# What runs in front of the first attention: masks before statistics, sums and differences on VectorE, the second half's sums within the loops, and another memory layout

## The chip, the cores and the metric

The kernel runs on one core of a Trainium2 chip. Its time is the device time in microseconds (us) of one execution. Three runs of the kernel before gave a median of 3515.47 us (3515.45 to 3517.23). Views of one profiled execution are quoted besides; the engines are PE (TensorE's matmuls; PEld its weight loads), DVE (VectorE), ACT (ScalarE), POOL (GpSimd) and SP (SyncE, which only issues DMAs here).

## The reference, cut to what matters

The whole program is a stack of layers on an image of 256 channels and 64 x 64 pixels: a group norm with a windowed linear attention (the part this document is about), a deformable convolution, two attentions and two mixtures of experts. The first attention computes, for 8 heads of 32 channels:

```
q = sigmoid(Wq x);  k = sigmoid(Wk x);  v = Wv x, each pixel's head vector divided by its length
Ik = integral image of k;  Ikv = integral image of k (outer product) v
for ws in 64, 32, 16:                # window of ws x ws pixels around each pixel, cut at the edge
    wk  = box(Ik, ws);  wkv = box(Ikv, ws)
    attn = q . wkv                   # 32 values per head and pixel
    norm = q . wk                    # one value per head and pixel
    outs.append(attn / (norm + 1e-6))
out = Wout concat(outs) + bout
```

x is the group-normalised image here.

## The kernel before, in words

Everything is done in two halves of 128 channels (4 heads), hf = 0 and 1. The image is cut into 8 blocks of 8 pixel rows (NBLK), 512 pixels each (NB).

*Masks* (`masks0`, line 248 on). Window membership is a product of a row vector and a column vector per mask. DVE computes the small vectors (`inside`, lines 282 and 283: two instructions per row or column of a mask), POOL multiplies them out to bf16 masks (lines 297, 301, 312, 327). `group_norm` (line 157 on) has DVE compute statistics of the image (16 `bn_stats`, line 166), a short chain of tiny operations over all engines gives mean and scale, and then DVE normalises the first 128 channels (line 172) and ACT the second (line 173) into y. Neither is in a hand-written order: a scheduler decides how the two mix on DVE.

*Preparation* (`prep0`, line 401 on), once per half, in an order written by hand for PE, DVE, ACT and POOL (`manual_schedule`):
- k of all 8 blocks: PE multiplies (line 146, a helper that all matmuls of this stage share), ACT applies the sigmoid twice, into the integral image T and into k (lines 413, 414), DVE scans along rows (line 422) and adds rows and blocks (line 418).
- a loop over the blocks nb. `ahead` takes T's row differences (line 478), window 16 on DVE and windows 64 and 32 on POOL. PE makes q of the next block and k and v of this one, pixels on partitions (kv); `keys` and `values` give v's length by ACT and DVE (lines 440 to 454). `weighed` takes column differences on DVE and multiplies by q (lines 496 to 501); `norms` sums them on PE into nrm (line 509). `tiles` multiplies k by v per tile of 8 x 8 pixels on PE, and ACT copies it to S (line 467). `sums` adds S over columns and rows on POOL, per block, with single 32- to 256-element additions (line 520), 10 to 16 per block.
- at the end, DVE takes the reciprocal of nrm (lines 566, 567); the sums go to DRAM (fard, neard; lines 548, 549), and the reciprocals too (recd, line 568).

POOL's sums of one half run until after its last block; DVE's reciprocal also.

*Attention* (`half0`, line 570 on), once per half, only PE's order written by hand. A first loop over u (8 columns of tiles, window 64) and a second over I (8 blocks). Per u it needs the state b from fard (block-diagonal tile bd, line 579, which must be zeroed once, line 383), the keys kt (kc, line 600), and v by columns (vt, line 377, 16 loads per half, from vd in DRAM). `region0` works through jobs, four for each u: PE multiplies scores (l_s, line 706) into six PSUM banks; of the four head products of a job DVE masks two straight from PSUM (line 718), ACT copies two (line 713) and POOL masks them with one multiplication (line 723); two jobs later PE multiplies them by vt (line 752), added to what the state gives (line 739).

Memory: the mask vectors' pool is freed before y's is made; y, the weights w_qk and w_kv, T and the constants share an area with what attention needs, so the weights are loaded, T's edges cleared and bd, vt loaded when the earlier users are through. SP and ACT issue the DMAs, each in its own order.

Of the kernel before, what the change touches and what calls it, by code (L numbers as in the profile page):

```python
# [88 lines left out]
class Net:  # L89
# [158 lines left out]
    def masks0(self, pool, tmp):  # L248
# [30 lines left out]
        def inside(out, d, at, ws):  # L279

            lo, hi = float(-(ws // 2) - at), float(ws // 2 - 1 - at)
            nc.vector.tensor_single_scalar(out, d, lo, ALU.is_ge)
            nc.vector.scalar_tensor_tensor(out, d, hi, out, ALU.is_le, ALU.mult)

        M = {}
        for ws, nr, n in ((32, 2, 10), (16, 1, 14)):
            rows = tmp.tile([P, 3, TR], F32, tag="rows", name="m_rows")
            cols = tmp.tile([P, 5, TCOL], F32, tag="cols", name="m_cols")
            for i, di in enumerate((-nr, 0, nr)):
                inside(rows[:, i], d_row, TR * di, ws)  # L290
            for j in range(5):
                inside(cols[:, j], d_col, TCOL * (1 - j % 3), ws)
            halves = cols.rearrange("p j (h c) -> p (j h) c", c=HC)
# [8 lines left out]


        rows = tmp.tile([P, 10, TR], F32, tag="rows10", name="m_rows")
        for i in range(10):
            inside(rows[:, i], d_tall, -TR * (i - 4), 64)
        cols = tmp.tile([P, 2, HC], F32, tag="cols2", name="m_cols")
        for s, du in enumerate((-4, 4)):
            inside(cols[:, s], d_half, HC * du, 64)
        full = pool.tile([P, 2, 10, TR, HC], BF16, tag="mask_c", name="mask_c")  # L310
        for s in range(2):
            nc.gpsimd.tensor_tensor(full[:, s], bc(rows, 3, HC), bc(bc(cols[:, s], 1, TR), 1, 10), ALU.mult)
        M["c"] = full.rearrange("p s i r c -> p s i (r c)")


        rows = tmp.tile([P, 2, TR], F32, tag="rows2", name="m_rows")
        for s, di in enumerate((-4, 4)):
            inside(rows[:, s], d_row, TR * di, 64)
        hf = tmp.tile([P, 1], F32, tag="hf", name="m_h")
        nc.vector.tensor_copy(hf, h_i)  # L320
        near = tmp.tile([P, 10], F32, tag="near", name="m_near")
        nc.vector.memset(near, 1.0)
        nc.vector.tensor_scalar(near[:, 0:2], hf.to_broadcast([P, 2]), 0.0, None, ALU.is_equal)
        nc.vector.tensor_scalar(near[:, 8:10], hf.to_broadcast([P, 2]), 0.0, None, ALU.is_gt)
        full = pool.tile([P, 2, 10, TR, HC], BF16, tag="mask_r", name="mask_r")
        for s in range(2):
            nc.gpsimd.tensor_tensor(full[:, s], bc(bc(rows[:, s], 1, 10), 3, HC), bc(bc(near, 2, TR), 3, HC), ALU.mult)
        M["r"] = full.rearrange("p s i r c -> p s i (r c)")
        return M

    def layer0(self, xc, x, xd, done):
# [4 lines left out]
        with tc.tile_pool(name="l0", bufs=1) as pool, tc.tile_pool(name="l0d", bufs=1, space=DRAM) as dpool:  # L336
# [7 lines left out]
            with tc.tile_pool(name="l0m", bufs=1) as tmp:  # L344
                M = self.masks0(pool, tmp)
            with tc.tile_pool(name="l0y", bufs=1) as ypool:
                y = ypool.tile([P, 2, N], F32, tag="y", name="l0_y")
                tiled = lambda a: a.rearrange("p (i u r c) -> p i r u c", i=NBLK, u=NU, r=TR)
                raster = lambda a: a.rearrange("p (i r u c) -> p i r u c", i=NBLK, r=TR, u=NU)
                self.group_norm(xc, lambda m: [(tiled(y[:, m])[:, i], raster(xc[:, m])[:, i]) for i in range(NBLK)])  # L350
                done()
                with (
                    tc.tile_pool(name="l0a", bufs=2) as wp,
                    tc.tile_pool(name="l0g", bufs=1) as gpool,
                    tc.tile_pool(name="l0a_ps", bufs=2, space=PSUM) as ps,
                ):
                    self.weights(ypool, ["w_qk0", "w_kv0"])
                    self.consts0(ypool)
                    T = gpool.tile([P, HW + 1, HW + 1], F32, tag="T", name="l0_T")
                    nc.gpsimd.memset(T[:, 0, :], 0.0)  # L360
                    nc.gpsimd.memset(T[:, 1:, 0:1], 0.0)
                    ET = mybir.EngineType
                    with tc.manual_schedule(engines={ET.PE, ET.DVE, ET.Activation, ET.Pool}):
                        for hf in range(2):
                            self.prep0(hf, y, q[hf], k[hf], None if hf else v, vd[hf], fard[hf], neard[hf], recd[hf], T, gpool, wp, ps)
            with (
                tc.tile_pool(name="l0o", bufs=1) as wop,
# [3 lines left out]
                vt = wop.tile([P, 4, NU, P], F32, tag="vt", name="l0_vt")  # L371

                def tall(hf):
                    by_rows = vd[hf].rearrange("(i b j) (h n) c -> b n i j h c", b=2, j=4, h=2)
                    for u in (4, 5, 6, 7, 0, 1, 2, 3):
# [3 lines left out]
                tall(0)  # L379
                self.weights(wop, ["w_out0"])  # L380
                bd = [[wp.tile([P, (NU, 4)[wi], P], F32, tag=f"bd{wi}{i}", name=f"l0_bd{wi}", bufs=1) for i in range(2)] for wi in range(2)]
                for b in bd[0] + bd[1]:
# [2397 lines left out]
```

## Time and profile before

| what | us |
|---|---|
| median of three runs | 3515.47 |
| the profiled execution | 3449.32 |
| its span, first to last instruction | 3447.3 |
| PE busy in the span | 3096.6 (90%) |
| DVE, POOL, ACT busy | 2302.0, 1566.5, 1319.1 |
| last statistic aggregated | 28.4 |
| first matmul of k | 35.2 |
| first S product of half 0, last one | 69.1, 130.9 |
| first S product of half 1, last one | 166.1, 227.2 |
| first score matmul of attention | 252.35 |

A line in order of time gives the start, the duration (of a run of equal instructions: from the first's start to the last's end), the engine, the line of the kernel, the operation, output <- inputs, the shapes and the count; in brackets stands how long the engine was idle just before, and what ended that. A line of windows gives, for a stretch, its length, each engine's busy time with its count of instructions, TensorE's granted clock (1.00 is full), the DMA engines' mean busy share and GB/s.

### The profile page before, as it was taken

To read this page: it belongs to the slowest core of one execution; us is meant where nothing else is said; L and a number is where in the kernel's file an instruction comes from. 1 tells how busy PE (TensorE), PEld (TensorE's weight loads), DVE (VectorE), ACT (ScalarE), POOL (GpSimd) and SP (SyncE) were. 2 spreads that over 40 slices of the span, in tenths; PEclk is the share of its full clock that TensorE was granted. 3 is DMA by queue.
4 is the path that set the end of the run, shared out by engine and by line. 5 is a ranking of instruction groups with operands and counts; after the bars stand their busy time and mean duration, and the time that the engine had idled before them with its cause. 6 is when DMAs were issued, how large, how long until landed. Compare 5 with 4: busy or idle time off the path is not lost.

```text
span 3447.3 us, 65631 instructions
## 1 busy us (share of the span) xinstructions
PE 3096.6 (90%) x25404; PEld 2321.3 (67%) x25404; DVE 2302.0 (67%) x5325; ACT 1319.1 (38%) x2537; POOL 1566.5 (45%) x1523
## 2 busy tenths in 40 slices
PE   5759999999977899797969789999999996999997
PEld 3433444344435888665857567888888885889996
DVE  7865776577764677797755576777777775555552
ACT  3435443443325666342533352222222222333331
POOL 3679887788752555443444352000000003555552
PEclk9879999999989999998979899999999997999998
DMA  1136655611134222200148653323333224555554
GB/s 68 43 90 143 173 151 154 156 52 52 52 110 123 61 74 74 57 1 1 56 166 264 214 192 123 103 87 96 101 99 98 90 64 158 195 193 203 206 203 174
DMA packets 241687, 406.97 MB, mean 118 GB/s; under 512 B 78353, under 2 KB 152850, under 8 KB 231890
## 3 DMA queue, kind: packets, MB, share of 16 engines
q1 hardware_dynamic: 212786, 345.19, 32.2%
q0 software_dynamic: 13056, 35.93, 2.7%
q10 hardware_dynamic: 15520, 21.52, 1.8%
q8 instruction: 204, 3.34, 0.4%
q14 instruction: 121, 0.99, 0.1%
HBM read 287.07 MB, written 111.30 MB: 116 GB/s over the span
## 4 chain that ended last, share of the span: by engine, by line
PE 40%; DVE 9%; DMA 5%; issue 5%; ACT 3%; POOL 3%; SPq 0%; DVEq 0%; POOLq 0%; ACTq 0%
PE a_sa_ps L2403 6%; PE f_h_ps L146 5%; DMA ys<-f_y,f_at 3%; PE a_oa_ps L2442 3%; PE a_ob_ps L2442 3%; PE a_oc_ps L2442 3%; PE a_sb_ps L2403 3%; PE f_ya_ps L146 2%; PE l_acc_ps L1097 2%; PE f_yb_ps L146 2%; PE a_od_ps L2442 1%; POOL ys L2158 1%; PE a_sc_ps L2403 1%; PE a_q_ps L146 1%; DVE l_pr L1093 1%
## 5 line engine op out<-in xcount | busy, mean ns | idle before, releaser
L713 ACT COPY l_sc<-l_s 128x384 f32<-128x384 f32 (+1 forms) x632 | 303.9, 532 | 459.9 <-PE l_s L706 434.2
L1971 POOL DMA_INDIRECT xs<-f_room,f_to x64 | 64.7, 1011 | 696.8 <-issue 582.2
L718 DVE TENSOR_TENSOR l_sm<-l_s,mask 128x256 f32<-128x256 f32 (+2 forms) x628 | 308.1, 552 | 91.2 <-PE l_s L706 90.3
L146 PE MATMUL f_h_ps<-f_xT,f_w 128*128 128x256 f32 x1440 | 339.8, 387 | 19.5 <-DVE f_xT L2078 9.6
L146 PEld LDWEIGHTS f_h_ps<-f_xT,f_w 128*128 128x128 f32 x1440 | 261.3, 191 | 83.1 <-ACT f_h L2088 31.8
L706 PE MATMUL l_s<-l_q,l_k 32*128 32x256 f32 (+3 forms) x2944 | 270.9, 453 | 0.0
L2422 ACT ACTIVATE a_e<-a_e 128x512 f32<-128x512 f32 x256 | 156.0, 629 | 243.2 <-DVE a_e L2392 237.9
L723 POOL TENSOR_TENSOR l_sm<-l_sc,mask 128x768 f32<-128x768 f32 (+1 forms) x116 | 202.8, 1755 | 87.7 <-ACT l_sc L713 87.5
L2088 ACT ACTIVATE f_h<-f_h_ps,f_w 128x256 f32<-128x256 f32 x360 | 166.3, 470 | 186.4 <-PE f_h_ps L146 177.1
L1093 DVE TENSOR_TENSOR l_pr<-l_vk,l_w_ps 128x1280 f32<-128x1280 f32 x128 | 186.6, 1482 | 54.1 <-PE l_acc_ps L1097 34.9
L706 PEld LDWEIGHTS l_s<-l_q,l_k 32*128 32x128 f32 x2944 | 132.7, 183 | 115.3 <-issue 68.3
L2158 POOL DMA_INDIRECT ys<-f_y,f_at x144 | 145.5, 1010 | 138.9 <-ACT f_y L2157 108.7
L1097 PE MATMUL l_acc_ps<-ident,l_pr 128*128 128x128 f32 x1600 | 198.1, 278 | 6.3 <-POOL l_pr L1088 6.2
L1097 PEld LDWEIGHTS l_acc_ps<-ident,l_pr 128*128 128x128 f32 x1600 | 184.7, 144 | 13.0 <-POOL l_pr L1088 7.8
L727 POOL TENSOR_TENSOR l_sm<-l_sc,mask 128x256 f32<-128x256 f32 (+1 forms) x220 | 184.8, 868 | 13.9 <-ACT l_sc L713 12.9
L2115 POOL TENSOR_TENSOR f_wt<-f_w 128x512 f32<-128x512 f32 x72 | 89.9, 1269 | 217.7 <-PE f_ya_ps L146 206.3
L2403 PE MATMUL a_sa_ps<-a_q,a_kt 128*128 128x256 f32 x512 | 155.8, 386 | 11.1 <-DVE a_u L2408 10.1
L2407 ACT COPY a_u<-a_sa_ps 128x256 f32<-128x256 f32 x128 | 47.6, 372 | 292.5 <-PE a_sa_ps L2403 292.5
L752 PE MATMUL l_b_ps<-l_sm,l_v 128*32 128x256 f32 (+2 forms) x2176 | 153.2, 372 | 0.0
L2403 PE MATMUL a_sa_ps<-a_qt,a_kt 128*128 128x256 f32 x512 | 152.7, 380 | 0.0
L723 POOL TENSOR_TENSOR l_sm<-l_sc,mask_c 128x768 f32<-128x768 f32 (+1 forms) x64 | 120.0, 1892 | 36.8 <-ACT l_sc L713 36.3
L2403 PE MATMUL a_sb_ps<-a_qt,a_kt 128*128 128x256 f32 x512 | 132.1, 381 | 0.0
(555 smaller groups left out, 7388.0 us busy)
## 6 DMA issues: line engine op xcount, KB each, us to landing
a_kt<-a_kd SPq DMA_DIRECT2D x128, 512.0 KB
f_w<-in_f_w SPq DMA_DIRECT2D x36, 1152.0 KB
f_w<-in_f_w SPq DMA_DIRECT2D x36, 1028.0 KB
xs<-zero SPq DMA_DIRECT2D x8, 4160.0 KB
l_vk<-vt SPq DMA_DIRECT2D x180, 128.0 KB
f_x<-xs SPq DMA_DIRECT2D x72, 260.0 KB
f_w<-in_f_w SPq DMA_DIRECT2D x36, 384.0 KB
l_rcp<-l_recd SPq DMA_DIRECT2D x48, 256.0 KB
```

The lines of the kernel that those rows point to most:

```text
L146: self.nc.tensor.matmul(out, lhsT, rhs, start=(i == 0), stop=(i == len(pairs) - 1))
L706: nc.tensor.matmul(s[pair, j][:, at : at + m, :], key(hp), qs[hp], start=(z == 0), stop=(z == len(pieces) - 1))
L713: nc.scalar.copy(sc[:, j], s[1, j])
L718: nc.vector.tensor_tensor(to(pair, j, kind, at), pick(s[pair, j], kind, which), mask, ALU.mult)
L723: nc.gpsimd.tensor_tensor(out[:, :, at, :], of[:, :, which, :], bc(mask, 1, 2), ALU.mult)
L727: nc.gpsimd.tensor_tensor(to(1, j, kind, at), pick(sc[:, j], kind, which), mask, ALU.mult)
L1093: nc.vector.tensor_tensor(pr, vk, bc(held["w"][:, j, dy], 3, D), ALU.mult)
L1097: nc.tensor.matmul(acc[:, m, j, :], pf[:, dx, m * P : (m + 1) * P], self.ident, is_transpose=True, start=(j == 0 and dy == 0 and dx == 0 a ...
L2088: nc.scalar.activation(h[:, m, :], q, AF.Gelu, bias=w1[:, 2 * hidden + m : 2 * hidden + m + 1])
L2158: nc.gpsimd.indirect_dma_start(out=self.ys_parts[(i % 4) * NI + k], in_=y[:, k, :], in_offset=None, out_offset=bass.IndirectOffsetOnAxis(a ...
L2403: mm = lambda out, i, right: nc.tensor.matmul(out, A[i], right, start=True, stop=True)
L2442: nc.tensor.matmul(out, vs[:, j, i, :], right, start=(j == 0 and side != 1), stop=(j == NPAIR - 1 and side != 0))
```

## The change

- The mask vectors are computed for several rows or columns at once (an index tile `x_i`, one `inside` with an outer sum), 48 DVE instructions in all, in a hand-written order in front of the statistics. POOL multiplies masks in another order (mask_c, mask_r, then 32 and 16). A dummy square root on ACT precedes everything.
- The weights have a pool of their own and are loaded at the start; T and the constants also have their own pools.
- In `prep0` all row differences are on DVE (before: two of three on POOL).
- `sums` becomes `sums0`: the same additions on DVE, for four blocks at a time: `columns(0)`, `columns(1)`, `rows`, `nears`. For half 0, `columns(0)` runs at block 5; the reciprocal and the other three run at the start of half 1's preparation. For half 1 all of them are handed on to attention (`more`), where the scheduler may place them: in the compiled order `columns(0)` stands within blocks 4 to 6 of the loop, and the rest on DVE before and between the masks of u = 0.
- k of half 1: the first four blocks are multiplied before the last S product of half 0 (`lead`), each gets one sigmoid, and ACT copies k into T.
- vt, bd and kc have a pool in y's old place; tiles of attention's second loop (rcp, o, xs) have one that is made when the sums' memory is free. One vt pair is loaded first, the rest and w_out in attention's first job. The sums' tiles stand at the other end of memory.

```diff
         for ws, nr, n in ((32, 2, 10), (16, 1, 14)):
...
-            for i, di in enumerate((-nr, 0, nr)):
-                inside(rows[:, i], d_row, TR * di, ws)
-            for j in range(5):
-                inside(cols[:, j], d_col, TCOL * (1 - j % 3), ws)
+            inside(rows, d_row, -TR * nr, TR * nr, ws)
+            inside(cols[:, :3], d_col, TCOL, -TCOL, ws)
...
-            with tc.tile_pool(name="l0m", bufs=1) as tmp:
-                M = self.masks0(pool, tmp)
...
+                self.weights(kpool, ["w_qk0", "w_kv0"])
...
-                self.group_norm(xc, lambda m: [(tiled(y[:, m])[:, i], raster(xc[:, m])[:, i]) for i in range(NBLK)])
+                with tc.tile_pool(name="l0m", bufs=1) as tmp, tc.manual_schedule(engines={ET.DVE, ET.Pool, ET.Activation}):
+                    root = tmp.tile([P, 1], F32, tag="root", name="m_root")
+                    nc.scalar.activation(root, self.one, AF.Sqrt)
+                    M = self.masks0(pool, tmp)
+                    self.consts0(kpool)
+                    T = tpool.tile([P, HW + 1, HW + 1], F32, tag="T", name="l0_T")
+                    nc.gpsimd.memset(T[:, 0, :], 0.0)
+                    nc.gpsimd.memset(T[:, 1:, 0:1], 0.0)
+                    self.group_norm(xc, lambda m: [(tiled(y[:, m])[:, i], raster(xc[:, m])[:, i]) for i in range(NBLK)])
                 done()
...
+                gpool = side.enter_context(tc.tile_pool(name="l0g", bufs=1, side="right"))
+                sums = self.sums0(gpool, fard, neard)
...
-                        for hf in range(2):
-                            self.prep0(hf, y, q[hf], k[hf], None if hf else v, vd[hf], fard[hf], neard[hf], recd[hf], T, gpool, wp, ps)
+                        lead = lambda: [self.channels0(1, y, k[1], i, C, ps) for i in range(4)]
+                        rest = self.prep0(0, y, q[0], k[0], v, vd[0], recd[0], T, sums, gpool, wp, ps, [], lead)
+                        rest = self.prep0(1, y, q[1], k[1], None, vd[1], recd[1], T, sums, gpool, wp, ps, rest, lambda: None)
...
+                        more = rest + [late] if hf == 0 else []
...
+        if hf == 1:
+            for i in range(4, NBLK):
+                channels(k, i, C)
+        for go in rest:
+            go()
         for i in range(NBLK):
-            channels(k, i, C, rows[:, i, :, 1:].rearrange("p r (u c) -> p r u c", c=HC))
+            if hf == 0:
+                channels(k, i, C, image(i))
+            else:
+                nc.scalar.copy(image(i), k.rearrange("p (i u r c) -> p i r u c", i=NBLK, u=NU, r=TR)[:, i])
...
-                    sub = (nc.vector if ws == 16 else nc.gpsimd).tensor_tensor
...
+                    nc.vector.tensor_tensor(d, hi, T[:, TR * (i - ni) : TR * (i - ni + 1)], ALU.subtract)
...
-            behind = [lambda nb=nb, vals=vals: tiles(nb, *vals), lambda nb=nb: sums(nb), lambda nb=nb, prs=prs: norms(nb, prs)]
+            if hf == 0 and nb == 5:
+                steps.pop(0)()
+            behind = [lambda nb=nb, vals=vals: tiles(nb, *vals), lambda nb=nb, prs=prs: norms(nb, prs)]
+        lead()
         for go in behind:
             go()
...
+        def reciprocals():
+            nc.vector.reciprocal(rec, rec)
+            nc.sync.dma_start(out=recd, in_=rec)
+        return [reciprocals] + steps
+
+    def sums0(self, pool, fard, neard):
+        plus = lambda o, a, b: nc.vector.tensor_tensor(o, a, b, ALU.add)
...
+            def columns(g):
+                at = slice(4 * g, 4 * g + 4)
+                a, o = S[:, at], R[:, at]
+                plus(pairs[:, at], a[:, :, 0::2], a[:, :, 1::2])
+                ends, two = o[:, :, 0:8:7], o[:, :, 1:7:5]
+                plus(ends, a[:, :, 0:5:4], a[:, :, 1:6:4])
+                plus(two, a[:, :, 2:7:4], a[:, :, 3:8:4])
+                plus(ends, ends, two)
+                for u in range(1, 4):
+                    plus(o[:, :, u], o[:, :, u - 1], a[:, :, u + 3])
+                    plus(o[:, :, 7 - u], o[:, :, 8 - u], a[:, :, 4 - u])
+            def rows():
+                ends, two = S[:, 0:8:7], S[:, 1:7:5]
...
+                nc.sync.dma_start(out=fard[hf], in_=S)
+            def nears():
+                plus(near[:, :7], pairs[:, :7], pairs[:, 1:])
+                plus(near[:, 7], pairs[:, 7], pairs[:, 6])
+                plus(near[:, 1:7], near[:, 1:7], pairs[:, :6])
+                nc.sync.dma_start(out=neard[hf], in_=near)
...
+            return S, [lambda: columns(0), lambda: columns(1), rows, nears]
...
             self.region0({"a": (HB, [(b[:, i, :], q4[:, i, u, :], i) for i in range(NBLK)])}, jobs, wp, ps, keep, go if u == 0 else None)
+            if more and u > 0:
+                more.pop(0)()
```

## The prediction

> **What bounds the kernel now.** I read the map of the span first, then busy time in windows at the stage boundaries, then the order in time on each engine. All instructions behind the first region loop keep their order on every engine (I compared both builds' instruction lists), so only about 0 to 267 us can change. The windows:
>
> ```profile
> 0.00:35.20 35.20, 1.14 (x4) 1.02 (x5) 26.79 (x109) 4.06 (x6) 17.61 (x38) 1.00 0.40 150
> 64.00:131.00 67.00, 47.35 (x621) 28.66 (x628) 60.78 (x136) 34.53 (x70) 53.23 (x99) 0.86 0.11 29
> 131.00:161.00 30.00, 29.84 (x146) 15.68 (x145) 23.79 (x26) 14.09 (x26) 7.51 (x18) 0.92 0.19 68
> 161.00:230.00 69.00, 49.63 (x676) 29.26 (x676) 60.78 (x136) 34.97 (x72) 55.70 (x104) 0.84 0.11 32
> 230.00:252.30 22.30, 0.00 (x0) 0.00 (x0) 4.95 (x3) 0.00 (x0) 7.17 (x17) 0.50 0.94 230
> 252.30:335.00 82.70, 81.95 (x1214) 31.09 (x1216) 46.05 (x79) 41.09 (x84) 71.95 (x38) 0.96 0.55 125
> ```
>
> The columns are busy PE, PE load, DVE, ACT, POOL, then granted clock and DMA. In front of attention DVE is the bound (60.8 of 67 us in each half's loop), PE is nearly idle until 35.2, and from 230 to 252.3 PE has nothing at all while the DMA engines are 94% busy. Then PE is full, and POOL busy 72 of 83 us.
>
> The order in time at the start and at the handover (start, duration):
>
> ```profile
> 6.00 5.03 DVE L166 BATCH_NORM_STATS2 gn_st<-xc 128x6 f32<-128x512 f32 x8 [5.04 <-DMA xc<-in_x]
> 23.76 4.24 DVE L166 BATCH_NORM_STATS2 gn_st<-xc 128x6 f32<-128x512 f32 x7
> 28.03 0.37 DVE L167 BATCH_NORM_AGGREGATE gn_mv<-gn_st 128x2 f32<-128x48 f32 x1
> 35.21 20.03 PE L146 MATMUL l_qk_ps<-l_y,w_qk 128*128 128x512 f32 x40 [3.97 <-DMA w_qk<-in_w_qk]
> ...
> 227.23 0.88 PE L146 MATMUL l_S_ps<-l_vb,l_kt 64*32 64x32 f32 x64 [6.84 <-DVE l_vb L454]
> 252.35 6.18 PE L706 MATMUL l_s<-l_q,l_kc 32*128 32x384 f32 x24 [22.38 <-DMA l_bd<-l_fard]
> ```
>
> Between the two statistics stretches DVE makes masks (11.0 to 23.8, less one statistic of 0.7: 12 us). At the handover PE waits for states written by POOL's last sums (done 235.5) and read back behind the vt loads.
>
> The sum is made on the profiled execution: span 3447.3, time 3449.32. The runs' median, 3515.47, is 66 us longer; which stages carry that is not shown, so I carry the saving over one to one.
>
> **Start: 8.6 us gained.** Mask vectors now precede the statistics: 48 DVE instructions from about 1.9 us (POOL's iotas end there), in a time in which DVE waited for the image until 6.0. Their cost:
>
> ```profile
> 11.06 0.14 DVE L261 TENSOR_SCALAR m_ri<-m_it 128x1 int32<-128x1 int32 x1
> 11.12 0.14 DVE L263 TENSOR_SCALAR m_ti<-m_it 128x1 int32<-128x1 int32 x1
> ...
> 30.24 0.16 DVE L186 TENSOR_TENSOR gn_dev<-gn_dev 128x2 f32<-128x2 f32 x1
> 30.43 0.16 DVE L187 TENSOR_TENSOR gn_dev<-gn_dev,gn_mv 128x2 f32<-128x2 f32 x1
> ```
>
> Independent ones start 0.06 to 0.07 apart, dependent ones 0.19. The Trainium skill (VectorE: DVE Perf Modes, "The DRAIN you can't avoid") measured that a semaphore between DVE operations costs nothing extra; by that, 48 x 0.07 = 3.4 us. The row is for operations this small and decides: 33 of the 48 wait for an earlier DVE one, 33 x 0.19 + 15 x 0.07 = 7.3. The last eight meet POOL's first mask products (1.27 us each): two blocked, 2.5. Statistics start at 11.7, take 16 x 0.61 + 2 x 0.3 = 10.4, end 22.1: 6.3 before today's 28.4. The square-root table load (30.70 to 31.98 on ACT, 0.55 behind the variance) goes under the image load: 0.55. The weights, issued at 30.21 today, are issued behind the image, so PE no longer waits from ACT's first y (33.43) to 35.21: 1.8. Sum 8.6. T's memsets and the head constants go to POOL ahead of T's first write and are hidden by the normalisation. Bounds: 12.5 if the skill's figure held, 5 if dependent ones took 0.3, some being 80 wide where the row has 2.
>
> **First half's loop: 2.7 gained.** Ten differences per half (four of window 64, six of window 32) go from POOL to DVE, at 0.73 each (L418, same shape, 14 in 10.27 us). What that buys is the shared port:
>
> ```profile
> 66.95 0.55 DVE L496 TENSOR_TENSOR l_e<-l_T 128x384 f32<-128x384 f32 x1
> 74.36 1.74 POOL L478 TENSOR_TENSOR l_d<-l_T 128x520 f32<-128x520 f32 x1
> 74.99 1.52 DVE L496 TENSOR_TENSOR l_e<-l_d 128x384 f32<-128x384 f32 x1
> ```
>
> With POOL still, 0.55; beside a POOL operation, the same shape ends 0.41 after POOL's end. With POOL empty I build an iteration from the first one's distances: 128x256 0.33, 0.21, 0.47 and so on, three differences 0.73: 7.5 us for blocks 4 to 7, 6.8 for blocks 2 and 3. PE's own period is 7.1 (last rows of S 0.69, nrm 0.98, qk 1.83, kv 3.62), so 7.3, 7.4, 7.8, 7.7. The sums of four blocks at once (ten instructions, 3.2 us) fall in block 5: 10.8. The first distance stays 9.4 (PE cold), the last is set by PE, which now has four key blocks in front of the last S: 0.69 + 0.98 + 4 x 1.72 = 8.6. From S of block 0 to S of block 7: 59.0 against 61.75 (69.14 to 130.89). Bounds -3 (durations stay) and +6 (all at PE's 7.1).
>
> **Between the halves: 5.4 lost.** From the last S to the first reduce is 30.0 us today (130.89 to 160.92), with POOL's sums beside the scans. Now DVE does it in order: nrm done 1.8, add 0.72, reciprocal 3.4, column sums 3.2, row sums 4.2, near sums 2.1 = 15.5 us; the eight scans at 1.21 = 9.7 (no longer paced by PE at 1.72, T being copied from k, on ACT by then), T's adds 10.27: 35.4. The fard, neard and recd writes leave here too, unread until the handover. Bounds -8 and -4.
>
> **Second half's loop: 3.9 gained.** As the first (61.1 to 57.2): 8.9 + 7.3 + 7.4 + 7.8 + 3 x 7.6, plus 3.0 for ten sums, which the scheduler puts singly into blocks 4 to 6. Bounds 0 and 7.
>
> **Handover: 13.8 gained.** bd, vt, kc fit in the place of y, so they load from the last kv matmul on, some 8 us before the last S; states are long in DRAM. PE can start 2.9 us after the last S (S 0.88, nrm 1.93) instead of 25.1. What is late next is DVE: in its queue, ahead of the first mask, stand pairs, column and near sums, the add and the 3.4 us reciprocal; and between the masks of u=0's four jobs 17 more sums. PE's second matmuls and its score banks wait for these masks. I count to the end of job 3's masks: today 262.31, 35.1 after the last S. New: S and its copies 1.4; 6.9 up to the reciprocal; masks 4.6 (1.02 + 1.29 + 1.29 + 1.02); 17 sums 6.75; one POOL mask product in the way, 1.65: 21.3. The DMA waits that the masks and ACT's copies get (the last vd write must have left the old buffer; w_out stands ahead of the copies on ACT) end by about 5, under the reciprocal. kc for u=2 stands behind the fard write on SP, which waits for those sums, at about 21; it is needed at about 27.
> Here a rule speaks against the change: the Trainium skill (SBUF — State Buffer, "Who interferes with whom") says a DVE instruction with two SBUF inputs waits for a whole GpSimd instruction that reads SBUF, and the row above shows it. POOL's products last 1.65 to 2.1 us here. If all of the four or five products that can have input by then block, 9.5 instead of 1.65: 29.2, gain 5.9. If DVE hid entirely, PE would set it: 2.9 + 10.0 (252.35 to 262.31), gain 22.2. I take 13.8, since POOL is fed by PE, which stands still while DVE is behind.
>
> **Sum:** 8.6 + 2.7 - 5.4 + 3.9 + 13.8 = 23.6. Profiled 3449.3 - 23.6 = 3425.7; median 3515.47 - 23.6 = 3491.9.
>
> **Rivals.**
> Full handover: sums slip into DVE's gaps, 22.2: gain 32.0, 3483.5. For: DVE has 46 of 83 us in the region; against: the order is fixed and the reciprocal stands first. 0.22.
> Heavy handover: 5.9: gain 15.7, 3499.8. 0.17.
> The change doesn't do what it says, no relief: DVE keeps today's durations and pays its 7.3 + 3.2 us per half, less the waits on POOL (about 2.5): loops -9.3 (with the four key blocks) and -8.0, gain about -0.3: 3515.8. Against: 0.42 against 0.67 for 128x256 without and with POOL. 0.04.
> Slower, the port at the handover: each of the 17 sums waits for a product of 1.85: 31.5 us, end at 51.1, so -16.0 there, in all -6.2: 3521.7. It turns to a loss from 25.3 us blocked, 14 products; PE, starved, cannot feed so many, hence 0.05; but a later u could carry the blocking on.
> The forecast: 0.52.
>
> Range: with the bounds of start and loops, 3479 to 3503 holds the forecast, full and heavy handover but for their ends. A difference under 0.2% (7 us) can't be told from none: faster 0.91, same 0.04, slower 0.05.
>
> **What would show it.** Right: second aggregate at about 22; PE's first qk at about 26.6; loop distances 7.3 to 7.8 with no L496 over 1 us; about 35 us between the halves; region start some 3 us after the last S, and job 3's masks 21 after it. Wrong if PE starts later than 30, if the loop stays near 9, or if PE stays gapped beyond u=1; or if more work per time lowers the granted clock later.

## The result, and the profile after

The changed kernel takes 3500.77 us (median of 5 runs, 3496.57 to 3501.27), the kernel before, run beside it, 3517.23 us (median of 5, 3515.45 to 3521.45). The ratio is 0.9949, 95% interval 0.9934 to 0.9963: about 16.5 us gained (18 by the ratio), with 13 to 23 us inside the interval. Forecast were 23.6 us, just beyond that interval, and 3491.9 us, with 3479 to 3503 as the range.

The two profiled executions can't be compared by their length: that of the changed kernel lasts 3496.57 us (span 3494.4), that of the kernel before 3449.32. Up to 1640 us the changed kernel is 17.3 us ahead; then the second attention, which the change does not touch, takes it some 64 us longer. The first experiment clears this up; up to there the traces compare instruction by instruction, and all that follows is read in front of it.

Busy time in windows of the changed kernel, at its own stage boundaries (columns as in the prediction: PE, PE load, DVE, ACT, POOL, granted clock, DMA share, GB/s):

```profile
60.40:121.00 60.60, 53.82 (x652) 31.53 (x655) 51.91 (x140) 33.39 (x68) 0.00 (x0) 0.91 0.13 36
121.00:155.30 34.30, 20.71 (x130) 11.96 (x118) 31.96 (x47) 10.99 (x22) 0.00 (x0) 0.87 0.14 52
...
217.00:221.00 4.00, 2.32 (x46) 0.54 (x37) 3.05 (x6) 0.43 (x2) 0.00 (x0) 0.50 1.03 228
221.00:302.20 81.20, 74.10 (x924) 25.87 (x925) 49.47 (x79) 32.74 (x67) 55.19 (x31) 0.87 0.56 136
```

GpSimd is empty in the first loop and between the halves (in the second half's loop it has only four memsets, 2.78 us, at the end), the gap of 22.3 us in front of attention has shrunk to 4, and VectorE is still the busiest engine between the halves. What is new is in the last line: in attention's first loop the clock is 0.87 where the window from 252.3 to 335 had 0.96 before, and PE is no longer full. Both come from the beginning of that window: from 268.8 to 302 us the clock is 1.00 and PE busy all the time, so the work that is moved forward does not lower the clock later.

The start and the handover, in order of time:

```profile
9.27 2.53 POOL L319 TENSOR_TENSOR mask_c<-m_rows,m_cols 128x640 bf16<-128x640 f32 x2 [6.50 <-DVE m_off L288]
9.30 1.29 DVE L290 TENSOR_TENSOR m_at<-m_d,m_off 128x16 f32<-128x16 f32 x1
...
22.28 0.37 DVE L167 BATCH_NORM_AGGREGATE gn_mv<-gn_st 128x2 f32<-128x48 f32 x1
...
221.02 7.41 PE L741 MATMUL l_s<-l_q,l_kc 32*128 32x384 f32 x24 [1.70 <-issue]
221.17 3.34 DVE L554 RECIPROCAL l_rec<-l_rec 96x512 f32<-96x512 f32 x1
226.98 4.96 DVE L563 TENSOR_TENSOR l_R<-l_R,l_S 128x128 f32<-128x128 f32 x5
227.41 4.38 POOL L758 TENSOR_TENSOR l_sm<-l_sc,mask_c 128x1024 f32<-128x1024 f32 x2 [1.10 <-ACT l_sc L748]
234.47 2.12 DVE L563 TENSOR_TENSOR l_S<-l_S 128x512 f32<-128x512 f32 x1
239.33 1.65 PE L741 MATMUL l_s<-l_q,l_kc 32*128 32x384 f32 x4 [3.77 <-DVE l_sm L753]
```

The first mask product of GpSimd stretches a VectorE operation of 0.17 us to 1.29, as forecast; the second aggregate ends at 22.65 and the first q matmul starts at 26.61. At the handover scores start 4.4 us after the last S, and then PE waits for VectorE, which has sums between its masks and GpSimd's mask products beside them.

Side by side, in us from the span's start (the third column is the experiment in which only the start is changed, told below; states of u=1 are the matmuls that bring in the state tile bd of that block of columns):

| landmark | before | start only | after |
|---|---|---|---|
| first q matmul | 35.21 | 26.62 | 26.61 |
| S of block 0, first half | 69.14 | 60.48 | 60.44 |
| S of block 7, first half | 130.89 | 121.6 | 120.84 |
| S of block 0, second half | 166.13 | 156.3 | 160.50 |
| S of block 7, second half | 227.23 | 217.41 | 216.59 |
| first score matmul | 252.35 | 242.00 | 221.02 |
| states of u=1 | 267.01 | 256.6 | 246.78 |
| states of u=3 | 283.7 | 273.3 | 268.8 |
| states of u=7 | 317.1 | 306.7 | 302.2 |

A second trace of the kernel before (first experiment) has u=1 1.6 us earlier than the first one and u=3 0.1 us, so a difference of 1 to 2 us at a single landmark says little.

The changed kernel is 10.6 us ahead at the last S, 31.3 at the first score, 20.2 at u=1 and 14.9 from u=3 on. It ends near 17.3: in the second half's attention, from u=2 to u=3, the kernel before takes 13.3 us (PE waits 3.48 for kc) and the changed one 10.4 (2.01). The edit leaves that stretch alone, and over the fourteen traces of this document it takes 10.4 to 15.0 us (12.6 in the second trace of the kernel before), so this part of the lead is luck of one trace. The stages behind shift by tenths.

The 5.3 us between u=1 and u=3 are the part of which the prediction knew nothing. SyncE's queue there, in the changed kernel:

```profile
240.01 0.36 SPq L591 DMA_DIRECT2D l_fard<-l_S  x1
...
241.16 1.49 SPq L597 DMA_DIRECT2D l_neard<-l_near  x1
246.90 1.22 SPq L626 DMA_DIRECT2D l_rcp<-l_recd  x2
...
251.25 1.54 SPq L818 DMA_DIRECT2D l_xs<-in_x  x2
252.84 4.76 SPq L612 DMA_DIRECT2D l_bd<-l_fard  x4
257.69 0.65 SPq L633 DMA_DIRECT2D l_kc<-l_k  x1
```

and what PE and ScalarE do at the same time:

```profile
259.65 2.06 ACT L748 COPY l_sc<-l_s 128x512 f32<-128x512 f32 x4 [4.67 <-DMA l_xs<-in_x]
260.29 0.91 PE L741 MATMUL l_s<-l_q,l_kc 32*128 32x384 f32 x2 [2.57 <-ACT l_sc L748]
262.54 1.66 PE L741 MATMUL l_s<-l_q,l_kc 32*128 32x384 f32 x8 [0.35 <-DMA l_kc<-l_k]
```

Two things stand out. SyncE has nothing to show between 242.7 and 246.9: the first loads into the memory over the sums (rcp, the reciprocals for attention's second loop; xs, the image, follows) come only after the fard and neard writes from that memory (it waits 1.4 us for the one to land and 2.8 for the other). And after the two xs loads the four state loads take 4.76 us to issue, 3.4 at this place before, kc for u=3 is issued 10.9 us after u=1's states (4.9 before, 271.94 against 267.01), ScalarE stands 4.67 us behind xs, and PE stops and then runs at a granted clock of 0.50 (262.5 to 264.2: 1.66 us for eight matmuls that take 0.93 from 268.8 on, at 1.00). These are 1.5 MB of loads, behind u=1's states now, and 1.5 MB of writes, issued 7 and 6 us ahead of them. In the kernel before the writes were done in the 22 us in which PE had nothing to do (issued at 232.3 and 235.6), and the four loads were issued from 253.3 to 263.4, in u=0, when states and kc of u=0 and u=1 had come in during those 22 us:

```profile
253.30 1.23 SPq L593 DMA_DIRECT2D l_rcp<-l_recd  x2
...
256.87 0.44 SPq L783 DMA_DIRECT2D l_xs<-in_x  x1
```

The second xs load follows at 263.00. Seen from u=1's states the four are 9 to 15 us later now. Which of these it is, the experiments have to tell.

### The profile page after: what moved, and what is told of

It reads as the page before. It is cut to its first block, busy times and chain, and to the rows that moved or that the text cites. A ratio compares the mean times of both kernels' runs of the same rounds, so it can differ in the third digit from the quotient of the medians.

```text
span 3494.4 us, 65430 instructions
## 1 busy us (share of the span) xinstructions
PE 3138.2 (90%) x25404; PEld 2347.2 (67%) x25404; DVE 2313.0 (66%) x5378; ACT 1319.1 (38%) x2538; POOL 1445.8 (41%) x1293
## 3 DMA queue, kind: packets, MB, share of 16 engines
q8 instruction: 204, 3.34, 0.4%
## 4 chain that ended last, share of the span: by engine, by line
PE 43%; DVE 8%; issue 6%; DMA 5%; ACT 3%; POOL 3%; SPq 0%; DVEq 0%; POOLq 0%; ACTq 0%
PE a_sa_ps L2438 6%; PE f_h_ps L146 5%; DMA ys<-f_y,f_at 3%; PE a_oa_ps L2477 3%; PE a_ob_ps L2477 3%; PE a_oc_ps L2477 3%; PE l_acc_ps L1132 3%; PE a_sb_ps L2438 3%; PE f_ya_ps L146 2%; PE f_yb_ps L146 2%; PE a_od_ps L2477 1%; DVE l_pr L1128 1%; PE a_sc_ps L2438 1%; POOL ys L2193 1%; PE a_q_ps L146 1%
## 5 line engine op out<-in xcount | busy, mean ns | idle before, releaser
L2438 PE MATMUL a_sa_ps<-a_q,a_kt 128*128 128x256 f32 x512 | 155.9, 386 | 13.4 <-DVE a_u L2443 12.6
```

The costliest lines, as they stand in the source:

```text
L2438: mm = lambda out, i, right: nc.tensor.matmul(out, A[i], right, start=True, stop=True)
```

## The experiments

They ran on several chips (the kernel before has medians of 3509.65, 3508.74, 3514.32 and 3452.78 us in the four comparisons), so only ratios to the before of the same comparison are compared, and landmarks of the traces. An interval of 0.0007 to 0.0015 on each side of a ratio is 3 to 5 us: most single steps are read from traces, one for each kernel, not from times. The edits are shown shortened.

### The kernel before once more

> The kernel before, unchanged, for its profile. Its first profiled execution lasted 3449.3 us and its timed runs 3515 to 3521; aligned with the changed kernel's profile, the 66 us lie in the second attention (about 1645 to 1745 us there), whose code the change doesn't touch. If that stage has two courses that an execution takes by its own timing, this profile shows either one: near 3515 with the tensor engine drip-fed there (4 to 5 matmuls, then a pause, 1.45 us apart), or near 3449 without. If the long course belongs to the changed kernel's instruction layout, this one lasts 3449 again, and the timed 3515 has another place.

3507.03 us, span 3505.0. At 1592 us it is within 0.1 us of the first profile, then the second attention takes 206.3 us (1632.7 to 1839.0) where the first profile has 147.2. So the long course is not the changed kernel's. It is in this kernel's own code, with TensorE's instructions arriving in drops:

```profile
1680.18 0.50 PE L1593 MATMUL a_s<-a_qT,a_vT 32*128 32x128 f32 x4 [0.45 <-issue]
1681.59 0.51 PE L1593 MATMUL a_s<-a_qT,a_vT 32*128 32x128 f32 x5 [0.91 <-issue]
```

Four or five matmuls every 1.43 us, behind nothing but issue. In the last comparison both kernels ran some 60 us shorter and the profile had the short course (148.0 us), so it goes with the chip or the occasion and not with the edit. What brings it about was not tried.

### The start alone

The kernel before with the new mask vectors and their order, the early weight load and the early table load; all the rest as before.

```
-  with tile_pool("l0m") as tmp: M = self.masks0(pool, tmp)
+  self.weights(ypool, ["w_qk0", "w_kv0"])
...
+  with tile_pool("l0m") as tmp, manual_schedule(DVE, Pool, Activation):
+      nc.scalar.activation(root, self.one, AF.Sqrt)
+      M = self.masks0(pool, tmp)        # the new form
+      self.consts0(ypool)
       self.group_norm(...)
```

> The kernel before with the start alone changed: mask vectors ahead of the statistics in their merged form, mask products behind, the weights' load and the square-root table early. Theory: TensorE's first q matmul comes 8.6 us earlier (26.6 instead of 35.2) and all stays 8.6 us earlier: 8 to 9 us less than the kernel before. Rival: the first loop is bound by VectorE and GpSimd, whose mask products now lie beside the image's sums; then 3 to 6 us of it is given back by the first S.

3500.2 us against 3508.74, ratio 0.9972 (0.9964 to 0.9979): 9.8 us by the ratio, 8.5 by the medians. The first q matmul is at 26.62, and the table above shows the lead kept: 8.7 us at the first S, 9.8 at the last, 10.4 at u=7. The forecast of 8.6 holds, and no contention takes it back. It is half or more of what the whole change gains (9.8 of 18 us by the ratios, 10.4 of 14.9 at u=7).

### Differences on GpSimd again

The changed kernel with one part undone.

```
+  ds = ahead(nb)        # windows 32 and 64 on gpsimd, at the head of the block
-  nc.vector.tensor_tensor(d, hi, T[...], ALU.subtract)
+  if ws == 16: make()   # on vector
```

> The changed kernel with one part undone: the differences of windows 32 and 64 are made on GpSimd again, ahead of the block, as in the kernel before. Theory (what the two engines do to each other through their shared port): VectorE's differences beside a running GpSimd operation go from 0.56 us to over 1 us, the loops of both halves get 2 to 4 us longer each: 3505 to 3508. Rival (VectorE is relieved of ten operations of 0.7 us per half, which outweighs it): 3495 to 3499.

3496.7 against 3508.74, ratio 0.9961 (0.9948 to 0.9974); the times alone don't separate it from the changed kernel's 0.9949. The traces do: 63.2 us from S to S in the first half instead of 60.4, 57.8 instead of 56.1 in the second, and with the longer way between them u=7 comes at 308.6 instead of 302.2 (1.0 us at the first S, 2.8 and 1.7 in the loops, 0.9 between them). Groups of VectorE in the second half's loop, first in the changed kernel (columns: busy us, mean ns | idle before):

```profile
L514 DVE TENSOR_TENSOR l_d<-l_T 128x520 f32<-128x520 f32 x17 | 11.8, 693 | 0.0
L518 DVE TENSOR_TENSOR l_e<-l_d 128x256 f32<-128x256 f32 x6 | 2.5, 422 | 0.1
```

and then in this one:

```profile
L514 DVE TENSOR_TENSOR l_d<-l_T 128x520 f32<-128x520 f32 x7 | 7.9, 1130 | 0.0
L532 DVE TENSOR_TENSOR l_e<-l_d 128x256 f32<-128x256 f32 x6 | 5.5, 916 | 0.0
```

Ten differences fewer on VectorE save 10 x 0.69 us; but those that stay take 1130 ns instead of 693, and the six subtractions behind them 916 instead of 422: 6.0 us more in these two rows alone. The theory's direction holds; of its 2 to 4 us for each loop the traces show 2.8 and 1.7.

### First half's sums on GpSimd, in the new form

```
-  plus = lambda o, a, b: nc.vector.tensor_tensor(o, a, b, ALU.add)
+  plus = lambda o, a, b: (nc.vector if hf else nc.gpsimd).tensor_tensor(o, a, b, ALU.add)
```

> The changed kernel with one part undone: the first half's sums (ten in block 5, the rest between the halves) are GpSimd's again, in the new form of four blocks at a time. Theory (moving sums to VectorE costs what they take there, when GpSimd beside it is idle): 3.2 us come off the first loop and up to 9.5 us off the 34.45 us between the halves, less what scans and adds lose beside GpSimd: 4 to 8 us gained in front of the second half. Rival (the port: each of VectorE's adds and differences waits for a whole GpSimd sum): 3 to 8 us lost there.

3502.49 against 3514.32, ratio 0.9961 (0.9946 to 0.9976). The rival is right: first S of the second half at 165.8 instead of 160.5. Of these 5.3 us 2.8 are lost in the first loop (63.2 us instead of 60.4), 2.3 between the halves and the rest ahead of the loop. Between the halves, VectorE's rows of this kernel:

```profile
133.87 15.00 DVE L458 TENSOR_TENSOR_SCAN l_T<-gate,l_T 128x520 f32<-128x520 f32 x8 [4.12 <-ACT l_T L456]
148.90 11.81 DVE L444 TENSOR_TENSOR l_T<-l_T 128x520 f32<-128x520 f32 x14
```

The scans of the changed kernel (its additions take 10.27 us):

```profile
135.91 9.16 DVE L458 TENSOR_TENSOR_SCAN l_T<-gate,l_T 128x520 f32<-128x520 f32 x8
```

The scans start 2 us earlier without the sums in front of them and end 3.8 us later: 1.88 us each beside GpSimd's sums of four blocks instead of 1.15.

### First half's sums on GpSimd, block by block

The same idea in the old form: small sums inside the loop, beside VectorE's own.

```
+  behind = [tiles(nb), block(nb), norms(nb)]   # block: the old sums of one block, on gpsimd
-  if hf == 0 and nb == 5: steps.pop(0)()
```

> The changed kernel with the first half's sums made as in the kernel before: on GpSimd, block by block inside the loop (differences stay on VectorE, the second half's sums stay in the new form). The last run had GpSimd make them four blocks at a time, in large operations, most of them between the halves, and lost 5.1 to 5.5 us. Theory (what GpSimd's sums cost VectorE depends on how many of them lie beside VectorE's work that needs the port; small ones inside a loop that has slack cost little, while 9.5 us of VectorE's time between the halves is saved): the first loop is 1 to 3 us longer, the time from the last S to the next reduce falls from 34.45 us to 25 to 28, first S of the second half at 154 to 156 instead of 160.5; about 5 us less than the changed kernel (3495 where it has 3500.8, ratio 0.9935). Rival (the port again): the loop grows by the 5 us that are saved, first S of the second half at 159 to 162, ratio 0.995.

3433.98 against 3452.78 (the chip with the short course), ratio 0.9949 (0.9936 to 0.9963), the same as the changed kernel's to four digits. The first loop takes 62.2 us instead of 60.4; from the last S to the next reduce 29.4 (122.6 to 151.96) instead of 34.45; first S of the second half at 157.2, 3.3 us earlier than in the changed kernel, u=7 at 298.6, 3.6 earlier. The direction is the theory's, the size two thirds. The missing 2 us are in one row:

```profile
132.58 9.17 DVE L458 TENSOR_TENSOR_SCAN l_T<-gate,l_T 128x520 f32<-128x520 f32 x8 [4.11 <-ACT l_T L456]
```

With the sums out of its queue VectorE waits 4.1 us for the copies of k on ScalarE. By the trace this is the best version in front of the second half; by the times it can't be told from the changed kernel, and at 677 us both traces stand at the same place, as its second half takes 4.3 us longer from u=2 to u=3 (14.7 against 10.4), the stretch that differs so much from trace to trace.

### No key blocks ahead of the last S

```
-  lead = lambda: [self.channels0(1, y, k[1], i, C, ps) for i in range(4)]
+  lead = lambda: None     # all eight blocks at the head of the second half
```

> The changed kernel with one part undone: the four key blocks of the second half are not put ahead of the last S of the first half, but stand behind it with the other four. Theory (TensorE, cold at that point, needs 8.7 us for them, so that the last distance between S was 11.3 instead of the forecast 8.6): the last distance falls to 8 to 9, and eight key blocks of 1.8 to 2.2 us lie under 15.5 us of VectorE's sums, so that nothing is given back: 2 to 3 us gained. Rival (the scans then wait for the keys' copies on ScalarE): the time between the halves grows by as much, no gain.

3499.97 against 3514.32, ratio 0.9962 (0.9947 to 0.9976). The last S comes at 117.5 instead of 120.84, a distance of 8.2 after 11.3, as the theory says; the first S of the second half comes at 160.6, where it was 160.5. The rival holds: the scans start at 136.02 after 2.45 us of waiting for ScalarE's copy of k, against 135.91 in the changed kernel. The 2.7 us by which the forecast of the last distance missed cost nothing in the end.

### Half 1's reciprocal behind u=0

```
+  if hf == 1: rec[:, 0:1] += 0 * mark     # mark: one element of u=0's copy
   nc.vector.reciprocal(rec, rec)
```

> The changed kernel, but the second half's reciprocal alone (3.34 us on VectorE ahead of the first mask) waits for the copy of attention's first block of columns, by a first operation that adds zero times that copy. Theory (VectorE's queue sets the handover): job 3's masks of u=0 end some 3.4 us earlier after the last S (21.5 instead of 25) and u=1's state matmuls come 3 us earlier; 3497 to 3498 if nothing is given back. Rival: those matmuls are set by loads (states and kc for u=1), and the norms, written out some 25 us later, hold the rcp load and all behind it in SyncE's queue: 3501 to 3506.

3493.64 against 3508.74, ratio 0.9949 (0.9936 to 0.9961). States of u=1 come at 241.69, 25.2 us after the last S. The changed kernel has 30.2 there, and two other runs with the same handover (no key blocks ahead; loads held until u=6) have 29.0, so 3.8 to 5 us are gained for 3.34 us taken out of VectorE's queue: VectorE sets the handover. Then, with the reciprocal at 243.39:

```profile
247.34 1.50 PE L746 MATMUL l_s<-l_q,l_kc 32*128 32x384 f32 x6 [1.21 <-DVE l_sm L758]
...
255.31 8.68 SPq L615 DMA_DIRECT2D l_bd<-l_fard  x4
```

u=1 to u=2 takes 12.5 us instead of 8.35, as PE waits for masks behind the reciprocal and then runs slowly (1.50 us for six matmuls), and u=3 to u=4 takes 11.9 as the states behind the xs loads need 8.68 us. At u=7 2.7 us are left, at 995 us 0.5. Both sides were partly right.

### Loads over the sums' memory held back, twice

Several runs hold operations back by writing one element that depends on a later copy. In three of them (this one and the two at the end) the element's own tile was put into the pool of vt, bd and kc.

```
+  mark = vpool.tile([P, 1], ...)
+  nc.scalar.copy(b[:, 0:1], mark)        # rcp, likewise xs, of row blocks 0 and 1
```

> The changed kernel, but the first loads into the memory that lies over the second half's sums (two rcp, two xs) are held back until the fifth block of columns of attention is done, by a one-element write of ScalarE into each tile. Theory: in the changed kernel these loads stand in SyncE's queue ahead of the output store, the v tile, the states and kc for u=3, and wait 4.3 us (242.65 to 246.90) for the fard and neard writes to land; that costs the 5.3 us lost between u=1 and u=3. It expects no such wait, kc for u=3 issued about 6 us after u=1's state matmuls instead of 10.9, and 3495 to 3497 against 3500.8. Rival: the 1.5 MB of writes themselves keep the DMA engines busy; they are written as before here, so it expects u=3 as late as in the changed kernel and 3500 to 3502.

3502.48 against 3509.65, ratio 0.9981 (0.9973 to 0.9988): slower than the changed kernel. u=2 to u=6 run at 8.35 us without a gap, though the writes are made too (issued at 240.25 and 245.14; 240.01 and 241.16 in the changed kernel): the rival, which blames the writes, falls. But u=7 comes 14.9 us after u=6, with one xs load issued at 291.27 in between and ScalarE idle for 5.24 us behind xs; and the first score matmul is late:

```profile
226.02 6.43 PE L747 MATMUL l_s<-l_q,l_kc 32*128 32x384 f32 x22 [6.97 <-DMA l_kc<-l_k]
```

vt, bd and kc fill y's 32 KB to the last byte (16 + 12 + 4). One more tile in that pool pushes kc past y's end, onto memory in use until the last S, and kc's load leaves after the last S (219.90, S at 216.31) instead of before it (207.73, S at 216.59): 5 us at the first score.

The same hold with the element in another pool, and until the copy of u=6:

> The changed kernel, but the first two rcp and the first two xs loads are held until the copy of u=6 (the last block but one), by a one-element write of ScalarE; the element that the hold is made from lies in the pool of working tiles, so that states, v and kc keep their places exactly over the memory of y. Theory: these loads, 1.5 MB in all, are what delays the states and kc of u=3; u=1 to u=7 take 50 to 51 us instead of 55.4, the first score matmul stays at 221, and 3495 to 3497 would stand where the changed kernel has 3500.8 (a ratio to the kernel before of about 0.9935 instead of 0.9949). Rival (the loads cost the same wherever they come): u=7 and the first row block of the next phase lose the 5 us again, ratio as before.

3503.63 against 3514.32, ratio 0.9967 (0.9955 to 0.9980). First score at 221.09, so the place of the element was what cost 5 us above. u=1 to u=7 takes 50.1 us (245.7 to 295.8), as the theory has it, and at u=7 it is 6.4 us ahead of the changed kernel (1.1 of them at u=1 already). They are lost again at the next row block, in the same form:

```profile
308.94 1.07 ACT L753 COPY l_sc<-l_s 128x512 f32<-128x512 f32 x2 [4.72 <-DMA l_xs<-in_x]
```

4.72 us where it was 4.67, with rcp and xs issued at 296.29 and 297.61 without any wait for memory. So it is neither the writes nor SyncE's 4.2 us of waiting for them: the loads cost this much in every place tried here. In the kernel before, where the states and kc of the next columns were in already, the same loads in u=0 cost less: 0.2 us in the first trace (u=0 to u=1 takes 8.55 us instead of 8.35), 1.5 in the second (9.81 from u=1 to u=2). Another 5.4 us are lost at 341; at least part of them is the hold's own doing, as ScalarE's element for a later rcp waits there 4.09 us for that tile.

### v of the second half on SyncE alone

```
-  (nc.sync, nc.scalar)[b].dma_start(out=vt[...])
+  (nc.sync, nc.sync if hf else nc.scalar)[b].dma_start(out=vt[...])
```

> The changed kernel, but the second half's v tiles, one for each block of columns, are loaded by SyncE alone instead of by SyncE and ScalarE in turn. The last runs moved the lost 5 us from u=2 and u=3 to wherever the two xs loads were put, with ScalarE each time idle behind xs for about 5 us while its own v load stands ahead of its score copies. Theory: the loss is that v load in ScalarE's queue, which waits for xs to land; with it on SyncE the copies go on, u=1 to u=7 take 50 us (six times 8.35) instead of 55.4, and the time is 3495 to 3497 against 3500.8. Rival: the loads themselves fill the DMA engines (281 GB/s and all 16 busy at 254 to 258 us) and kc for u=3 comes late whatever queue v stands in, with more to issue on SyncE: 3500 to 3504.

3490.23 against 3508.74, ratio 0.9949 (0.9935 to 0.9964): no change by the times. ScalarE no longer stands behind xs, but u=3 comes at 268.1 (268.8), u=1 to u=7 takes 56.7 us where the theory had 50, the states behind the first xs load take 4.36 us to issue, and PE waits for kc:

```profile
260.64 1.66 PE L741 MATMUL l_s<-l_q,l_kc 32*128 32x384 f32 x8 [3.89 <-DMA l_kc<-l_k]
```

The theory of ScalarE's queue falls. Whoever stands behind the xs load in time waits, ScalarE's v or SyncE's states and kc; from 258 to 262 us the DMA engines are 98% busy at 258 GB/s.

### The second half's sums behind u=0

The reciprocal and all sums of the second half, held back by the same kind of element (in the pool of kc again, so the first score starts at 223.87 and not at 221).

```
+  if hf == 1:
+      rec[:, 0:1] += 0 * mark;  S[:, 0::4, 0, 0:1] += 0 * mark
```

> The changed kernel, but the second half's reciprocal and sums wait for the copy of attention's first block of columns (u=0), by a first operation that adds zero times that copy. Theory (the handover's size is set by VectorE's queue): reciprocal and sums leave the path between the last S and the first masks; the masks of u=0's four jobs end about 11 to 14 us after the last S instead of 24, the second half's loop loses its ten sums (3 us), and u=1's state matmuls come 10 to 13 us earlier. The writes then meet SyncE's queue later and the 5 us at u=2 to u=4 stay lost: 3488 to 3491. Rival (the work is only moved to where the mask products of GpSimd block it, and the masks wait there instead): 3498 to 3503.

3510.97 against 3509.65, ratio 1.0003 (0.9995 to 1.0011): the whole gain is gone. The masks of u=0 end 15 to 16 us after the last S (at 230.8) instead of 24, so the sums do stand in their way at the handover. But then (the first row is one of sums that nothing blocked):

```profile
254.71 1.28 DVE L567 TENSOR_TENSOR l_R<-l_R,l_S 128x128 f32<-128x128 f32 x6
...
281.17 10.16 SPq L616 DMA_DIRECT2D l_bd<-l_fard  x4
```

From 247 to 272 VectorE works on the reciprocal and sums with a mask in between: u=1 to u=3 takes 31.2 us instead of 22, and u=4 to u=5 another 7.3 over 8.35, as the states behind rcp and xs take 10.16 us to issue.

And with the loads held back too:

```
+  rec, S: as above, behind the copy of u=0
+  rcp, xs of row blocks 0 and 1: behind the copy of u=5
```

> Both of the last two edits: sums and reciprocal of the second half behind u=0's copy, first loads into their memory behind the copy of u=5. If both theories hold, 10 to 13 us and 4 to 5 us: 3483 to 3487. If only the queue of VectorE matters, as the run with the sums held back; if neither, 3500.

3513.77 against 3509.65, ratio 1.0013 (1.0006 to 1.0020). The loads' 4 to 5 us are not gained: it is no faster than the run before. u=1 to u=3 takes 31.3 us as above, and with the loads held until u=6 the loop goes on at 8.35 up to u=7, but then PE stops 2.83 us behind ScalarE's copies. Its first score is late by the same accident (225.36). These two runs show that the place at the handover, bad as it looks in VectorE's queue, is the cheaper one for the sums (of the 8.6 us by which the first is behind the changed kernel at u=3 at most some 4 are its late first score). Probably it is because there they lie partly in front of the first mask, where VectorE would wait for PE anyway (in the run with the reciprocal alone held back it is idle for 1.20 us before that mask with sums ahead of it).

## Why the prediction was right, and where it was not

**Start, 8.6 us: right, 8.60 at the first q matmul.** In parts, the second aggregate comes 5.75 us earlier (forecast 6.3), the chain from there to the first y is 0.79 us shorter (0.55) and PE's wait behind that 2.06 us (1.8): small misses that cancel. The 48 mask instructions run from 1.79 to 12.39, 10.6 us, of which 2.5 are the two that meet GpSimd's products: 8.1 for the rest, where the rows gave 7.3. By the Trainium skill (VectorE: DVE Perf Modes, "The DRAIN you can't avoid"), where a semaphore between operations costs nothing extra, the estimate was 3.4. For operations this small the row was the one to follow.

**First half's loop, +2.7: 61.75 became 60.4, +1.35.** Blocks 1 to 6 run as worked out or faster (8.6, 7.4, 7.2, 7.9, 7.4, 10.5); only the last distance is 11.3 instead of 8.6, since PE, after a wait of 5.12 us, needs 8.7 us for four key blocks that were put at 6.9, and 1.93 for the norms' matmuls that were put at 0.98. Taking the blocks away gives 3 us there and nothing further on, so the term was wrong without a price.

**Between the halves, -5.4: 34.45 against 30.03, -4.4.** The two runs with sums on GpSimd show the choice behind it: in large pieces, in the loop and beside the scans, they cost 5.3 us more than on VectorE, in small pieces inside the loop 3.3 us less. By these traces moving half 0's sums is a loss; first loop and gap together lose 3.1 us against the kernel before, and it is the second half's loop that makes up for it.

**Second half's loop, +3.9: 61.1 became 56.1, +5.0.** With GpSimd still, durations are those of the quiet rows (0.42 and 0.56), and the run with differences on GpSimd shows what they become otherwise. Start apart, all this nets 1.9 us by the last S (forecast 1.2), and against the run of the start alone 0.8, which is less than two traces of one kernel can differ.

**Handover, +13.8: 11.3 at the prediction's own mark, 9.6 at u=1.** Job 3's masks end 23.8 us after the last S, forecast 21.3 and before 35.1. The term mis-sized is the single GpSimd product that was counted in the way, 1.65 us: the rows show five column sums taking 4.96 us where six take 1.28 in the run with all sums held back, and a row sum of 2.12 instead of 0.68, so some 5.3 us were blocked, while the other terms together came out about a microsecond shorter than counted. That is the Trainium skill's rule (SBUF — State Buffer, "Who interferes with whom") nearer than the middle value that was taken, though not at the forecast's worst case of 9.5. That VectorE's queue is the bound there is shown by the reciprocal's run. From these masks to u=1's states it takes 6.4 us where it took 4.7: PE, just out of its waits, needs 1.94 us for eight matmuls that take 1.06 later on. The prediction had no term for that.

**The step that failed** is one that the prediction made in two sentences: kc for u=2 stands behind the fard write, "at about 21; it is needed at about 27", and with that SyncE's queue was done. Of kc for u=2 this was right (issued 23.9 us after the last S, and no wait of PE's for it). But the first rcp and xs loads were neither costed nor moved in the sum. Their memory is now the sums', so they can't start before the sums are written out, and with the scores 31 us earlier they fall behind u=1's states, between the loads for u=2 and for u=3, where they fell into u=0 before. At u=3 5.3 of the 20.2 us are given back: PE stays gapped beyond u=1, which the prediction had named as a sign of being wrong. The held-back loads show that the price, 3.6 to 7.3 us in the runs, is the loads' own and comes wherever attention is running and the states and kc of the next columns stand behind them. A late kc could be read in the kernel before: in its second half SyncE stands 7.9 us at an xs load, and PE then waits 3.48 us for the kc behind it.

**Rivals.** Full handover is excluded by u=1's states, and slower port too. Heavy handover gave about the right total (15.7) by another way: 3.4 us of the 23.6 are missing at u=1, where the masks are 2.5 late, 5.3 more are lost to the loads by u=3, and 2.4 come back in the second half's attention, by luck: 17.3. That only 0 to 267 us can change holds for the order of instructions and not for their times. "No relief" falls with the loop rows.

**What stays open:** the second half's sums were not tried on GpSimd, nor the memory layout by itself. And what within the DMA makes the states and kc wait so long behind 1 MB of xs, whether the bytes or an order among transfers, was not separated; a run with the same loads cut to a few bytes would leave tiles unwritten and was not tried.

## What to carry to other kernels

When memory is laid out anew, list every transfer into the memory that changes its owner, the lines that the diff doesn't touch too, and say after which write it can now start and which loads it will then meet. Look some steps beyond the first instruction that benefits: here the gain was 31 us at the first score, 20 at u=1 and 15 at u=3. And take a change apart on the chip: half or more of this one's gain comes from its start, small vector work put into a wait for the image.

## What was not expected

- A stage far away from the edit has two courses, 147 and 206 us long, that go with the chip or the occasion; TensorE then gets four or five instructions every 1.43 us. A profile of one course and times of the other (3449 and 3515 us) had to be compared for this prediction; a difference of profiled spans would have shown the change 47 us slower.
- One more tile of four bytes per partition in a pool that exactly fills freed memory costs 5 us, as the load of kc is then held until the last S.
- Eight scans beside GpSimd's sums take 15.00 us instead of 9.16, a larger stretch than that of the additions behind them (11.81 instead of 10.27).
